# A fourth tile of score operands, the second half of a block loaded one patch sooner, and shared tiles that make room

## The chip, the cores and the metric

The kernel runs on one core of a Trainium2 chip. The metric is the device time of one execution in microseconds (us); for the kernel before it is the median of three executions.

A core has five engines that matter here: TensorE (PE, matrix products; PEld are its weight loads), VectorE (DVE), ScalarE (ACT), GpSimd (POOL) and SyncE (SP), which in this kernel only issues DMA transfers. Each engine takes its instructions strictly in order, and waits for other engines through semaphores. SyncE's queue issues nearly all transfers, so a transfer that has to wait there holds up all that stand behind it.

## The reference, cut to what matters

The input x has shape (8, 512, 2048), the context the same. A layer takes x through gated cross attention, then through a mixing of four streams:

```python
x = x + tanh(g_xattn) * xattn(layernorm(x), ctx, mask, ...)
x = x + tanh(g_ffn) * ffn(layernorm(x), ...)
```

The attention works on patches of 128 columns. Queries and keys both come from the normalized x, values from the context:

```python
q = einsum('ed,bdw->bew', Wq, qp) + bq      # per patch: 256 rows, 128 columns
k = einsum('ed,bdw->bew', Wk, qp) + bk
scores = einsum('bhdi,bhdj->bhij', qh, kh) / sqrt(32)   # 8 heads of 32 rows
attn = softmax(where(mask, scores, -1e9))
o = gelu(einsum('bhij,bhdj->bhdi', attn, vh))
out = (Wo @ o + bo) * mask
```

The mixing normalizes every row again, takes 24 logits per row from it, runs 50 Sinkhorn iterations on a 4 x 4 matrix per row, and combines the four 512-wide streams of the row with that matrix and with one 512 x 512 product.

## The kernel before, in words

**Tiling.** The 2048 columns of each of the 8 batches are cut into blocks of 512 columns (n = 0 to 31 over all batches), a block into 4 patches of 128 (p = 0 to 3, t = 4n + p), and, for the score operands, into two halves of 256 columns (m = 2n and 2n + 1). A half serves two patches.

**The score operands.** `proj(n)` (L261) normalizes a block, and computes queries and keys on TensorE in four groups of 128 rows (L288 to L290). ACT and DVE split each group into a high and a low half-precision part `ev` (L294, L295), and SyncE writes it to a scratch tensor `qd` in memory (L296). `stack(m)` (L301) loads one half back into a tile QK in the layout that the score products want: three transfers (L308 and twice L313, 768 KB together) and one row of the mask (L318). There are NS = 3 such tiles; half m goes to tile m mod 3, so its load waits until the scores of half m - 3 have been read. Three more rows of each tile are constants or row maxima: the constants are written once in the setup from `crow` (L401 to L404), the maxima by a small transfer per patch (L359, `mh`).

**The scores.** `smax(t)` (L339) multiplies queries and keys of patch t (L346, 8 matmuls), takes row maxima on DVE (L349 to L352), transposes them (L354), and writes them back into the QK tile (L356, L359). `expo(t)` (L626) makes the transposed scores with the maxima subtracted (L633, called sT) and ACT takes the exponential (L635). `attv(t)` (L638) multiplies with the values (L650, L654), which `vproj` (L328) makes from the context (`ct`, L326; L336). `outp(n)` (L660) takes a finished block through Gelu, the mask tile `mb` (L668, L669), a transposed copy `gT` (L672, L673, L679, L680) that is summed with weights into `g4` (L683) and `g4s` (L685), the output product (L705 to L708), the residual (L709) and the store to x1s (L712).

**The mixing.** `rawmap(b)` (L717) turns the sums of a finished batch into logits (among it `las`, L740, L741, and its transposes `lt`, L744), `ffn` runs the Sinkhorn iterations on DVE and POOL (L878 to L899), `mixv` combines the streams on ACT, POOL and DVE (L947 to L992; it passes products in the single buffer `pj`, L961, L984), and `mixp` does it on TensorE for fifteen of the 32 row groups (L995 to L1050), all after the main loop (the tail). Its four output tiles per group, `wp`, alternate between one buffer `eh` and two of `e32` (L1048), and are stored through ACT's queue (L1050).

**What sets the order.** The main loop runs over t, and for each t over the letters of ORDER. At each letter `act` (L1084) emits a piece of work. `smax` runs four patches ahead of `expo`. `stack(2(n+2))`, the first half of block n + 2, is emitted at p = 3 of block n just after the last group of its projection (L1138, L1139); `stack(2(n+1)+1)`, the second half of block n + 1, at p = 2 of block n (L1103, L1104). These calls give a priority; a scheduler with a model of the time line then fixes each engine's order of instructions when the kernel is built. It moves instructions past each other where tiles and semaphores allow. So a small edit can move instructions on all engines. Pools of tiles limit it: where a pool has one buffer for a tag, the next tile of that tag waits for the last reader of the one before.

The lines named are those of the kernel before.

Of the kernel before, what the change touches and what calls it, by code (L numbers as in the profile page):

```python
# [9 lines left out]
F32 = mybir.dt.float32  # L10
F32R = mybir.dt.float32r
F16 = mybir.dt.float16
# [7 lines left out]
P = 128  # L20
D = 512
S = 2048
DK = 256
NH = 8
DH = 32
BLK = 512
NBLK = S // BLK
NP = BLK // P
SB = 256
NSB = BLK // SB  # L30
PSB = SB // P
NS = 3
HI = 1000
XPRE_POOL = lambda b: b < 7
AHEAD = 3
# [26 lines left out]
BUF_W = 2  # L62
BUF_X1 = 2
BUF_PJ = 1
BUF_PH = 1
BUF_EP = 2
# [32 lines left out]
def gated_xattn_mhc_kernel(  # L99
# [21 lines left out]
    V, A, G, T, SY = nc.vector, nc.scalar, nc.gpsimd, nc.tensor, nc.sync  # L121
# [24 lines left out]
    WqkH = ctile([P, 4, 512], F16, "WqkH")  # L146
    WqkL = ctile([P, 4, 512], F16, "WqkL")
    Wv = ctile([P, 4, DK], F32, "Wv")
# [4 lines left out]
    Wm = ctile([P, 16, 32], F32, "Wm")  # L153
# [9 lines left out]
    maskT = ctile([P, B * 16], F32, "maskT")  # L163
# [27 lines left out]
    ep = ctx.enter_context(tc.tile_pool(name="ep", bufs=BUF_EP))  # L191
# [6 lines left out]
    VF = [ctile([P, 2, DK], F32, f"VF{i}") for i in range(NV)]  # L198
# [164 lines left out]
    with tc.tile_pool(name="set", bufs=1) as st:  # L363

        def stile(shape, dt, name, tag=None):
            return st.tile(shape, dt, tag=tag or name, name=name)
# [31 lines left out]
        ctload(0)  # L398
        SY.dma_start(bvc, bv.rearrange("(g p) -> p g", p=P))
        for val, rows in ((NEG, [t[96:97] for t in QS]), (-M_UNIT, [r for t in KS for r in (t[97:98], t[98:99])])):  # L400
            crow = stile([1, NH, SB], F16, f"crow{int(val)}")  # L401
            V.memset(crow, val)
            for r in rows:
                SY.dma_start(r, crow)  # L404
        tgx = stile([P, 1], F32, "tgx")
        A.activation(tgx, gx, AF.Tanh)
        A.activation(tgf, gf, AF.Tanh)
# [91 lines left out]
        pj = proj(1)  # L499
# [60 lines left out]
    lnp = ctx.enter_context(tc.tile_pool(name="lnp", bufs=3))  # L560
    op_ = ctx.enter_context(tc.tile_pool(name="op", bufs=BUF_OP))
    gp = ctx.enter_context(tc.tile_pool(name="gp", bufs=BUF_GP))
    fp = ctx.enter_context(tc.tile_pool(name="fp", bufs=2))
# [96 lines left out]
    def outp(n):  # L660

        b, k = divmod(n, NBLK)
        o = ob.pop(n)
        for g in range(2):
            gi = A.activation(o[:, g], o[:, g], AF.Gelu, bias=bvc[:, g : g + 1])
        with tc.issue_after(gi.ins), tc.high_priority():
            A.preload_act_table_set(EXP_SET)
        mb = gp.tile([P, BLK], F32, tag="mb", name="mb")  # L668
        SY.dma_start(mb, mask[b, k * BLK : (k + 1) * BLK].partition_broadcast(P))  # L669
        G.tensor_tensor(o, o, mb.unsqueeze(1).broadcast_to([P, 2, BLK]), ALU.mult)  # L670
        j0 = n * NP
        gt_ = op_.tile([P, NP, DK + 1], F32, tag="gT", name="gT")  # L672
        G.tensor_copy(gt_[:, :, DK], maskT[:, j0 : j0 + NP])  # L673
        yield
        for q in range(2):
            pt = ps_t.tile([P, 2, 2, P], F32, tag="t", name="gTp")
            for j in range(2):
                for e in range(2):
                    T.transpose(pt[:, j, e, :], o[:, e, (2 * q + j) * P : (2 * q + j + 1) * P], ident)  # L679
            V.tensor_copy(gt_[:, 2 * q : 2 * q + 2, 0:DK], pt.rearrange("p j e s -> p j (e s)"))  # L680
        g4 = ps_t.tile([P, DK + 1], F32, tag="t", name="g4")
        for p in range(NP):
            T.matmul(g4[32 * p : 32 * p + 32, :], Wm[:, k * NP + p, :], gt_[:, p, :], start=True, stop=True)  # L683
        if k == 0:
            g4s = lnp.tile([P, DK + 1], F32, tag="g4s", name="g4s", bufs=2)  # L685
            V.tensor_copy(g4s, g4)
            G4[b] = g4s
        else:
            V.tensor_tensor(G4[b], g4, G4[b], ALU.add)
        mr = MR[n % 2]  # L690
        SY.dma_start(mr[0:6, :], mrow_d[:, n * BLK : (n + 1) * BLK])
        gh = gp.tile([P, 2, BLK], F32R, tag="gh", name="gh")
        A.copy(gh, o)
        gl = gp.tile([P, 2, BLK], F32R, tag="gl", name="gl")
        G.tensor_tensor(gl, o, gh.bitcast(F32), ALU.subtract)  # L695
        if k == 0:
            sq2[b] = lnp.tile([P, 4, NBLK], F32, tag="sq2", name="sq2")
            x1s[b] = x1d.tile([D, S], F32, tag="x1s", name="x1s")
        xt = xtile.pop(n)
        yield  # L700
        for c in range(4):
            ps = ps_p.tile([P, BLK], F32, tag="p", name="op")
            cs = slice(c * P, (c + 1) * P)
            for e in range(2):
                T.matmul(ps, WoH[:, e, cs], gh[:, e], start=(e == 0), stop=False)  # L705
                T.matmul(ps, WoH[:, e, cs], gl[:, e], start=False, stop=False)  # L706
                T.matmul(ps, WoL[:, e, cs], gh[:, e], start=False, stop=False)
            T.matmul(ps, bo6[:, cs], mr, start=False, stop=True)  # L708
            V.tensor_tensor(xt[c], ps, xt[c], ALU.add)  # L709
            jk = fp.tile([P, BLK], BF16, tag="ph", name="junk2", bufs=BUF_PH)  # L710
            A.activation(jk, xt[c], AF.Square, bias=nmean[b][:, c : c + 1], accum_out=sq2[b][:, c, k : k + 1])  # L711
            defer(D_X1, "x1", lambda cs=cs, c=c: SY.dma_start(x1s[b][cs, k * BLK : (k + 1) * BLK], xt[c]))  # L712
            yield
# [3 lines left out]
    def rawmap(b):  # L717

        gtp = ps_t.tile([P, 3, 32], F32, tag="t", name="gtp")
        for e in range(2):  # L720
            T.matmul(gtp[:, e, :], G4[b][:, e * P : (e + 1) * P], sel, start=True, stop=True)
        T.matmul(gtp[0:3, 2, :], G4[b][:, DK : DK + 1].broadcast_to([P, 3]), sel, start=True, stop=True)
        gth = f1.tile([P, 2, 32], F32R, tag="gth", name="gth")
        V.tensor_copy(gth, gtp[:, 0:2, :])
        gtl = f1.tile([P, 2, 32], F32R, tag="gtl", name="gtl")
        V.tensor_tensor(gtl, gtp[:, 0:2, :], gth.bitcast(F32), ALU.subtract)
        ch3 = f1.tile([3, 32], F32R, tag="ch3", name="ch3")
        V.tensor_copy(ch3, gtp[0:3, 2, :])
        cl3 = f1.tile([3, 32], F32, tag="cl3", name="cl3")
        V.tensor_tensor(cl3, gtp[0:3, 2, :], ch3.bitcast(F32), ALU.subtract)  # L730
        V.tensor_scalar(cl3, cl3, cs3[:, 1:2], None, ALU.mult)
        c3 = f1.tile([3, 32], F32R, tag="c3", name="c3")
        V.scalar_tensor_tensor(c3, ch3.bitcast(F32), cs3[:, 0:1], cl3, ALU.mult, ALU.add)
        la = ps_t.tile([32, 512], F32, tag="t", name="la")
        for e in range(2):
            T.matmul(la, gth[:, e, :], WoH[:, e, :], start=(e == 0), stop=False)
            T.matmul(la, gth[:, e, :], WoL[:, e, :], start=False, stop=False)
            T.matmul(la, gtl[:, e, :], WoH[:, e, :], start=False, stop=False)
        T.matmul(la, c3, bor, start=False, stop=True)
        las = ep.tile([P, 512], F32, tag="eh", name="las", bufs=1)[0:32, :]  # L740
        A.copy(las, la)  # L741
        lt = ps_t.tile([P, 4, 32], F32, tag="t", name="lt")
        for c in range(4):
            T.transpose(lt[:, c, :], las[:, c * P : (c + 1) * P], ident[:32, :32])  # L744
        rw = lnp.tile([P, 4, 34], F32, tag="raw", name="raw")
        V.tensor_tensor(rw[:, :, 0:32], lt, rawx[b], ALU.add)
        V.tensor_reduce(rw[:, :, 32], sq2[b], AX.X, ALU.add)
        V.tensor_copy(rw[:, :, 33], nmean[b])
        raws[b] = rw
# [245 lines left out]
    def mixp(b, n, maps, inp=False):  # L995
# [9 lines left out]
        for g in range(4):  # L1005
            q = 4 * n + g
# [10 lines left out]
        pt = (ps_t if inp else ps_p).tile([P, 4, P], F32, tag="t" if inp else "p", name="xpT")  # L1017
# [25 lines left out]
        for g in range(4):  # L1043
            q = 4 * n + g
            ps = ps_t.tile([P, 512], F32, tag="t", name="mx1") if inp else pw[g // 2][:, g % 2]
            T.matmul(ps, QD[:, 32 * g : 32 * g + 32].rearrange("p t i -> p (t i)"), ys, start=True, stop=False)  # L1046
            T.matmul(ps, HD[:, g].rearrange("p t i -> p (t i)"), xc[g], start=False, stop=True)  # L1047
            w = fp.tile([P, 512], F32, tag="w", name="w", bufs=BUF_W) if inp else ep.tile([P, 512], F32, tag="eh" if g % 2 else "e32", name="wp", bufs=1 if g % 2 else BUF_EP)  # L1048
            A.activation(w, ps, AF.Identity, bias=rec[:, q, 2:3])
            A.dma_start(orow[q * P : (q + 1) * P, :], w)  # L1050
            yield 1

    NT_ = NTOT * NP
    mixq, tailq = [], []
# [29 lines left out]
    def act(c, t):  # L1084
        n, p = divmod(t, NP)
# [12 lines left out]
        elif c == "P" and live_ and n + 1 < NTOT:  # L1098
            if p == 0:
                at("proj", run, pj_[0])  # L1100
            if (SP0 == 0 or n == 0) and p == 0:
                at("stack", stack, NSB * (n + 1))
            if p == 2:  # L1103
                at("stack", stack, NSB * (n + 1) + 1)  # L1104
        elif c == "l" and live_:
            if p == LXP and n > 1 and n + 3 < NTOT:
# [127 lines left out]
```

## Time and profile before

| what | value |
|---|---|
| median of three executions | 1650.96 us (1650.79 to 1660.62) |
| the profiled execution | 1660.9 us |
| its span, first to last instruction | 1659.1 us |
| granted clock of TensorE, mean | 0.966 |
| busy: TensorE, DVE, ACT, POOL | 1481.3, 1160.3, 1061.5, 798.7 us |
| bytes moved by DMA | 330.55 MB, mean 199 GB/s |

The profile comes from one further execution. Busy time of an engine is the time in which it carried out an instruction; the rest it waited. A line such as `PE smax L346 <- DMA QK<-qd: 21.5, 12, 5.8` says that TensorE's instruction of line 346, which writes the tile smax, had to wait for the transfer that fills QK from qd: 21.5 us in all, 12 times, 5.8 us at the longest. In a time line the columns are start (us from the span's start), duration, engine, line, operation, tiles and shapes, count, and in square brackets the engine's idle time before it and what ended it. Lines of SPq are issues: their duration is that of the issue, not of the transfer.

### The profile page before, as it was taken

How to read it: one execution, taken by the hardware profiler on the slowest of the kernel's cores; microseconds unless marked ns; L12 is line 12 of the kernel's file. 1: busy time of each engine (PE TensorE's matmuls, PEld its weight loads, DVE VectorE, ACT ScalarE, POOL GpSimd, SP SyncE). 2: the span in 40 equal slices, each digit the busy share in tenths (PEclk: the TensorE clock that was granted, in tenths of full speed). 3: DMA queues.
4: the chain of work that ended last, by engine and by line, in shares of the span. 5: the costliest groups of instructions: out<-in, count | busy, mean ns of one | idle time of the engine just before them, and what ended most of it. 6: DMA issues, size and time to landing. Idle time of an engine off the chain costs nothing.

```text
span 1659.1 us, 31662 instructions
## 1 busy us (share of the span) xinstructions
PE 1481.3 (89%) x10524; PEld 887.6 (53%) x10589; DVE 1160.3 (70%) x3513; ACT 1061.5 (64%) x1924; POOL 798.7 (48%) x1149
## 2 busy tenths in 40 slices
PE   4798999999999988989897998888899999699998
PEld 2455556665656655555554565555565656433333
DVE  7454434665677578867886788876898878678772
ACT  3357466767667666777677766686677665655564
POOL 1321423444554454646675664667567744433221
PEclk8999999999999999999998998999999999899999
DMA  5688886687568755986678756896566565154653
GB/s 192 154 248 247 251 280 186 179 255 231 169 204 233 241 178 167 257 266 198 176 225 241 226 177 182 240 280 191 160 178 200 165 190 141 53 169 153 184 167 134
DMA packets 258179, 330.55 MB, mean 199 GB/s; under 512 B 43543, under 2 KB 143191, under 8 KB 258014
## 3 DMA queue, kind: packets, MB, share of 16 engines
q1 hardware_dynamic: 248078, 312.44, 63.7%
q10 hardware_dynamic: 9936, 16.06, 2.6%
q8 instruction: 84, 1.38, 0.4%
q14 instruction: 81, 0.66, 0.1%
HBM read 226.71 MB, written 101.16 MB: 198 GB/s over the span
## 4 chain that ended last, share of the span: by engine, by line
PE 36%; DMA 20%; DVE 18%; ACT 11%; issue 8%; POOL 6%; SPq 2%; POOLq 0%; ACTq 0%; another core or an unknown queue 0%; DVEq 0%
DMA xs<-in_x_dram 4%; DMA QK<-qd 4%; DMA xTt<-in_xT_dram 3%; PE vp L336 3%; DVE w L988 3%; PE mx L1046 3%; DMA qd<-ev 3%; PE mx L1047 3%; DVE smax L349 2%; PE op L705 2%; PE qk L288 2%; PE xpp L1012 2%; PE qk L289 2%; PE qk L290 2%; DMA out_dram<-w 2%
## 5 line engine op out<-in xcount | busy, mean ns | idle before, releaser
L336 PE MATMUL vp<-Wv,ct 128*128 128x256 f32 x1024 | 249.0, 398 | 15.2 <-DMA ct<-in_cx_dram 7.8
L336 PEld LDWEIGHTS vp<-Wv,ct 128*128 128x128 f32 x1024 | 202.3, 201 | 49.8 <-issue 9.9
L888 POOL TENSOR_TENSOR W<-E,uv 128x64 f32<-128x64 f32 x343 | 117.4, 346 | 203.3 <-DVE uv L886 100.4
L288 PE MATMUL qk<-xh,WqkH 128*128 128x512 f16 x512 | 196.1, 384 | 13.2 <-DVE ev L295 8.3
L349 DVE TENSOR_REDUCE smax<-smax 128x8 f32<-128x1024 f32 x128 | 155.8, 1217 | 65.0 <-PE smax L346 63.6
L276 POOL TENSOR_TENSOR xl<-xn,xh 128x512 f16<-128x512 f32 x126 | 153.9, 1221 | 97.3 <-ACT xh L274 92.3
L289 PE MATMUL qk<-xl,WqkH 128*128 128x512 f16 x512 | 196.3, 383 | 3.9 <-POOL xl L276 3.9
L290 PE MATMUL qk<-xh,WqkL 128*128 128x512 f16 x512 | 196.2, 383 | 0.0
L882 POOL TENSOR_TENSOR W<-E,uv 128x64 f32<-128x64 f32 x308 | 106.7, 350 | 175.0 <-DVE uv L892 76.0
L635 ACT ACTIVATE e<-sT,ebi,esc 128x1024 f32<-128x1024 f32 x128 | 153.2, 1197 | 40.4 <-PE sT L633 40.1
L988 DVE SCALAR_TENSOR_TENSOR w<-x,Et,w 128x512 f32<-128x512 f32 x153 | 151.1, 989 | 22.6 <-POOL w L986 11.9
L271 POOL TENSOR_SCALAR xn<-xt,ln_r,nb 128x512 f32<-128x512 f32 x126 | 107.9, 856 | 117.5 <-DVE nb L255 53.1
L890 DVE TENSOR_REDUCE sm<-W 128x16 f32<-128x64 f32 x392 | 99.7, 257 | 83.5 <-POOL W L888 79.5
L711 ACT ACTIVATE junk<-xt,nmean 128x512 bf16<-128x512 f32 x128 | 91.6, 716 | 76.1 <-DVE xt L709 41.6
L705 PE MATMUL op<-gh,WoH 128*128 128x512 f32 x256 | 117.3, 460 | 24.9 <-DVE ev L295 12.4
L294 ACT ACTIVATE ev<-qk,bqs 128x512 f16<-128x512 f32 x128 | 86.4, 676 | 75.8 <-PE qk L290 75.4
L346 PE MATMUL smax<-QK 97*128 97x128 f16 x1024 | 84.4, 225 | 45.9 <-DMA QK<-qd 26.2
L295 DVE SCALAR_TENSOR_TENSOR ev<-qk,bqs,ev 128x512 f16<-128x512 f32 x128 | 93.2, 729 | 42.9 <-ACT ev L294 34.4
L709 DVE TENSOR_TENSOR xt<-op,xt 128x512 f32<-128x512 f32 x128 | 86.5, 676 | 37.0 <-remote 20.6
L884 DVE TENSOR_REDUCE sm<-W 128x16 f32<-128x64 f32 x352 | 73.1, 211 | 56.0 <-POOL W L882 52.5
L346 PEld LDWEIGHTS <-QK 97*128 97x128 f16 x1024 | 67.2, 100 | 76.2 <-DMA QK<-qd 33.4
L706 PE MATMUL op<-gl,WoH 128*128 128x512 f32 x256 | 103.7, 405 | 0.2 <-POOL gl L695 0.2
(288 smaller groups left out, 3451.6 us busy)
## 6 DMA issues: line engine op xcount, KB each, us to landing
xt<-in_x_dram SPq DMA_DIRECT2D x64, 512.0 KB
ct<-in_cx_dram SPq DMA_DIRECT2D x64, 512.0 KB
qd<-ev SPq DMA_DIRECT2D x128, 256.0 KB
QK<-qd SPq DMA_DIRECT2D x64, 512.0 KB
xTt<-in_xT_dram SPq DMA_DIRECT2D x64, 512.0 KB
x1s<-xt SPq DMA_DIRECT2D x128, 256.0 KB
xs<-in_x_dram SPq DMA_DIRECT2D x56, 512.0 KB
x<-x1s SPq DMA_DIRECT2D x34, 512.0 KB
```

Of the source, the lines that this page charges most:

```text
L271: G.tensor_scalar(xn, xt[c], rstd1[b][:, c : c + 1], nb1[b][:, c : c + 1], ALU.mult, ALU.add)
L276: (V if n == 0 and c > 1 else G).tensor_tensor(l, xn, h, ALU.subtract)
L288: T.matmul(ps, WqkH[:, c, ms], hs[c], start=(c == 0), stop=False)
L289: T.matmul(ps, WqkH[:, c, ms], ls[c], start=False, stop=False)
L290: mm = T.matmul(ps, WqkL[:, c, ms], hs[c], start=False, stop=(c == 3))
L336: T.matmul(ps[:, h, :], ct[:, c, h * P : (h + 1) * P], Wv[:, c, :], start=(c == 0), stop=(c == 3))
L346: T.matmul(sc[:, h, :], q[0:97, h, sl], kk[0:97, h, sl], start=True, stop=True)
L349: V.tensor_reduce(mx, sc, AX.X, ALU.max)
L635: A.activation(e32, sc, AF.Exp, bias=ebi[:, t : t + 1], scale=esc[:, t : t + 1])
L705: T.matmul(ps, WoH[:, e, cs], gh[:, e], start=(e == 0), stop=False)
L888: (G if SK_POOL(b - B + 8) else V).tensor_tensor(W4[:, h], E4[:, h], ub[:, h], ALU.mult)
L988: V.scalar_tensor_tensor(w, x1[j], E[:, n, 4 * j + i : 4 * j + i + 1], w, ALU.mult, ALU.add)
```

## The change

The kernel after has four QK tiles instead of three, so half m goes to tile m mod 4 and waits for half m - 4. The second half of a block is emitted at p = 1 instead of p = 2. A QK tile takes 8 KB of every partition, and the room for the fourth is made in these places:

- `crow` is one row of 256 columns, and the transfer repeats it for the 8 heads;
- `gT` is cut in two tiles of two patches each; the second shares the buffer of `mb`, which grows by 8 bytes a partition;
- `g4s` has one buffer instead of two;
- `las` uses the buffer of `pj`;
- the tag `eh` is gone: `mixp` writes its outputs in turn to five tiles that the main loop no longer needs (parts of the weights WqkH, WqkL and Wv, and both value tiles VF) and to two buffers of `e32`.

```diff
-NS = 3
+NS = 4
...
-            crow = stile([1, NH, SB], F16, f"crow{int(val)}")
+            crow = stile([1, SB], F16, f"crow{int(val)}")
             V.memset(crow, val)
             for r in rows:
-                SY.dma_start(r, crow)
+                SY.dma_start(r, crow.unsqueeze(1).broadcast_to([1, NH, SB]))
...
-        mb = gp.tile([P, BLK], F32, tag="mb", name="mb")
+        mb = gp.tile([P, 2 * (DK + 1)], F32, tag="mb", name="mb")[:, :BLK]
         SY.dma_start(mb, mask[b, k * BLK : (k + 1) * BLK].partition_broadcast(P))
         G.tensor_tensor(o, o, mb.unsqueeze(1).broadcast_to([P, 2, BLK]), ALU.mult)
         j0 = n * NP
-        gt_ = op_.tile([P, NP, DK + 1], F32, tag="gT", name="gT")
-        G.tensor_copy(gt_[:, :, DK], maskT[:, j0 : j0 + NP])
+        gt_ = [op_.tile([P, 2, DK + 1], F32, tag="gT", name="gT"), gp.tile([P, 2, DK + 1], F32, tag="mb", name="gT1")]
+        for q in range(2):
+            G.tensor_copy(gt_[q][:, :, DK], maskT[:, j0 + 2 * q : j0 + 2 * q + 2])
...
-            V.tensor_copy(gt_[:, 2 * q : 2 * q + 2, 0:DK], pt.rearrange("p j e s -> p j (e s)"))
+            V.tensor_copy(gt_[q][:, :, 0:DK], pt.rearrange("p j e s -> p j (e s)"))
...
-            T.matmul(g4[32 * p : 32 * p + 32, :], Wm[:, k * NP + p, :], gt_[:, p, :], start=True, stop=True)
+            T.matmul(g4[32 * p : 32 * p + 32, :], Wm[:, k * NP + p, :], gt_[p // 2][:, p % 2, :], start=True, stop=True)
         if k == 0:
-            g4s = lnp.tile([P, DK + 1], F32, tag="g4s", name="g4s", bufs=2)
+            g4s = lnp.tile([P, DK + 1], F32, tag="g4s", name="g4s", bufs=1)
...
-        las = ep.tile([P, 512], F32, tag="eh", name="las", bufs=1)[0:32, :]
+        las = fp.tile([P, 512], F32, tag="pj", name="las", bufs=BUF_PJ)[0:32, :]
...
-            w = fp.tile([P, 512], F32, tag="w", name="w", bufs=BUF_W) if inp else ep.tile([P, 512], F32, tag="eh" if g % 2 else "e32", name="wp", bufs=1 if g % 2 else BUF_EP)
+            w = fp.tile([P, 512], F32, tag="w", name="w", bufs=BUF_W) if inp else tailw(g)
...
+    spare = [WqkH.bitcast(F32)[:, 0:2, :], WqkL.bitcast(F32)[:, 0:2, :], Wv[:, 0:2, :], VF[0], VF[1]]
+    turn = [0]
+
+    def tailw(g):
+        k = turn[0] % (len(spare) + 2)
+        turn[0] += 1
+        if k < len(spare):
+            return spare[k].rearrange("p c e -> p (c e)")
+        return ep.tile([P, 512], F32, tag="e32", name="wp")
...
-            if p == 2:
+            if p == 1:
                 at("stack", stack, NSB * (n + 1) + 1)
```

## The prediction, made before the changed kernel had run

> **What bounds the kernel now.** I read the page first, then the waits of TensorE and of SyncE's queue, then the time line of single blocks on both.
>
> ```profile
> span 1659.1 us, 31662 instructions
> PE 1481.3 (89%) x10524; PEld 887.6 (53%) x10589; DVE 1160.3 (70%) x3513; ACT 1061.5 (64%) x1924; POOL 798.7 (48%) x1149
> ...
> PEclk8999999999999999999998998999999999899999
> ```
>
> TensorE is busy for 89% of the span, so the change can only win what lies in its 178 us of idle time, and lose what it adds there. The windows by 100 us put 35 us of that idle time into the first 100 us, about 123 us into 100 to 1400, 14 us around 1400 to 1500 and nearly none into the tail. In 100 to 1400 the waits of TensorE are these (us, times, longest):
>
> ```profile
> PE smax L346 <- DMA QK<-qd: 21.5, 12, 5.8
> PE op L705 <- DVE ev L295: 12.4, 10, 2.5
> PE g L683 <- DVE gT L680: 9.1, 6, 3.3
> PE lgx L577 <- DMA xTt<-in_xT_dram: 8.8, 6, 4.5
> ```
>
> The largest is the wait for the score operands, which the change is about. SyncE's queue waits for the same tiles, because a tile must be free before it is loaded (over the whole span):
>
> ```profile
> SPq L308 <- DMA qd<-ev: 32.1, 24, 3.8
> SPq L308 <- PE sT L633: 26.2, 12, 5.4
> SPq L313 <- PE sT L633: 16.1, 11, 3.5
> ```
>
> Which half of a block is waited for? The time line of SyncE, then of TensorE, around the longest such wait:
>
> ```profile
> 902.70 0.64 SPq L308 DMA_DIRECT2D QK<-qd  x1
> 903.38 0.59 SPq L313 DMA_DIRECT2D QK<-qd  x1
> 904.07 0.39 SPq L326 DMA_DIRECT2D ct<-in_cx_dram  x1
> 904.55 0.93 SPq L612 DMA_DIRECT2D xs<-in_x_dram  x2
> 910.42 0.62 SPq L308 DMA_DIRECT2D QK<-qd  x1
> 911.09 1.07 SPq L313 DMA_DIRECT2D QK<-qd  x2
> ```
> ```profile
> 908.52 1.01 PE L346 MATMUL smax<-QK 97*128 97x128 f16 x8 [5.76 <-DMA QK<-qd]
> 909.33 1.06 PE L633 MATMUL sT<-QK 99*128 99x128 f16 x8
> ...
> 926.07 0.61 PE L346 MATMUL smax<-QK 97*128 97x128 f16 x8 [0.68 <-ACT e L635]
> ```
>
> The first half (issue at 902.70) stops TensorE for 5.76 us. The second half is issued at 910.42, just after the sT group at 909.33 has freed its tile, and its first smax starts at 926.07, 15.6 us later and not held by that load. I paired every L308 issue with the first smax group of its tile in this way. All waits of smax for QK<-qd lie at first halves. From block 4 on, first halves start 5.5 to 10.5 us after the issue (13 of 28 under 6.6), second halves 7.8 to 19.9 us (mean 13.1). A load alone lands in 5.5 to 6 us, so every second half already has at least 2 us to spare.
>
> **The change part by part.** The profiled execution took 1660.9 us (span 1659.1 and 1.8 around it), 0.6% over the median of 1650.96; the terms below are a few us, so I take them off the median unscaled.
>
> *Second half a patch sooner, fourth tile.* TensorE's waits at second halves come to 0.3 us (one, for the mneg row at 681.7). Gain: 0 to 0.3, taken as 0. The freed queue time (26.2 + 16.1 + 6.8 for L318, 49 us of SyncE standing at a load until sT frees a tile) is SyncE's: what stood behind it has slack (mh rows below). Zero.
>
> What the loads move past: in the built programs I counted what stands on SyncE between the first and the second half's L308. Before: 34 ct, 29 x1s, 14 xs, 14 MR, 14 out, 11 xTt, 11 mb, 10 x1, 6 qd, 4 mh. After: 15 x1s, 8 xTt, 6 out, 6 x1, 3 mh. So some 110 transfers now come behind three more issues (0.63 + 2 x 0.50 = 1.6 us) and 768 KB (3.8 us at the page's 199 GB/s). ct is waited for once only, in the setup; xs costs ACT 33.0 us in 19 waits, and 14 x 3.8 = 53 us more at the very most, on an engine that is 64% busy; TensorE's waits for ACT's e after it are 4.9 us. I take 0, bound +5.
>
> What stands ahead of the first half: those waits depend on it. With 260 to 522 KB issued in the 6 us ahead, first halves landed after 5.8 us (t=80, 32, 112, 120); with 1542 KB after 8.95 (t=64): 3.1 us per 1000 KB. With 1664 KB issued in the 3 us *behind* it (t=80) it still took 5.83, so the second half behind the first doesn't slow it. Between the last qd write and the first half's L308 stand 504 KB on average before and 414 after; in the four issues ahead of that write 1053 and 989. That is 90 to 150 KB less, 0.3 to 0.5 us on each of the 16 blocks in which TensorE waits there: 4.5 to 7.5 us. Only part reaches the end, since DVE's waits follow: -3, bounds -8 to +8 (the order may as well put more in front; other waits are re-dealt too).
>
> On this point the Trainium skill ("DMA: Bandwidth & Descriptors", section "Queues, rings and completion order") says that on each DMA engine a queue's descriptors are consumed in ring order. It speaks against the change: the 768 KB moved up don't go any faster and everything behind has to let them by. By the rule alone the first half gains nothing from a sooner second half and the sum would have 0 for -3; t=80 agrees that what is behind doesn't matter.
>
> TensorE's own order hardly moves: priced by the mean time of each line, the work between a block's last projection matmul and the first smax at p=0 is 15.1 us before and 14.9 after. So the cover of the first half is as thin as it was.
>
> *Setup.* Two memsets of 2048 columns (1.765 us each) become 256 (0.22 by ratio): 3.1 us less on DVE before 5.3 us; but the last x tile is waited for until 18.4. DVE's order also changes: wq is scaled before the last statistics, and WqkL (4.73) stands ahead of the chain to nb (0.9). ACT's WqkH (4.76) starts at 22.0 to 23.6 instead of 25.24; WqkL ends 31.5 to 33.1 instead of 34.76; then nb, xn 0.77, xl 1.15: first L289 at 34.3 to 35.9 instead of 35.63, since POOL's xl no longer runs beside WqkL (4.31 then, 1.15 elsewhere). Taken -0.5; bounds -2 and +2 (WqkH no sooner: the chain waits for WqkL). Three more constant rows: 3 x 0.55 us on SyncE, which is idle from 33 to 43.9. Zero.
>
> *Two gT tiles, one in mb's buffer.* 32 more copies on POOL at 0.19: 6 us on an engine 48% busy, covered by it; bound +6. The next mask load now waits for the g matmuls instead of o's multiply, which end 8.4 us later on average (3.9 to 14.2). It stands a little later on SyncE; behind it is mostly mh (20 of the next two rows in the loop). From block 4 to the last but one, mh is issued 13 to 47 us ahead of its sT; that covers 8.4. Zero; without that cover it is the time of the rival below.
>
> *g4s with one buffer:* rawmap has read it a block earlier. Zero, at worst 8 copies of 0.42. *las in pj's buffer:* of the 8 copies three would find pj in use (616.04 until 617.47, 800.18 until 803.47, 991.22 until 991.79); with las 0.57 long, the transposes at 802.36 would start 1.7 us later and the others about in time. Taken +1, bounds 0 and +5.
>
> *Tail output in seven buffers instead of three:* ACT waits 9.4 us for its own output transfers, TensorE 3.5 (weight loads) for ACT; but the windows 1500 to 1600 show TensorE busy for 100 of 100. Only the last 10 us can win: -1, bounds 0 and -3.5.
>
> Sum: 0 - 3 - 0.5 + 1 - 1 = -3.5, so 1650.96 - 3.5 = 1647.5 us. Within 1% is about what a measurement can't tell from no change: 1634.5 to 1667.5.
>
> **The rivals.**
> *Faster:* the waits at first halves go as well, because the scheduler uses the fourth tile to have first halves loaded ahead. For: they are TensorE's largest wait (21.5 in the loop, 4.6 in the setup). Against: they end with the qd write (SPq L308 <- DMA qd, 24 times), which the change leaves where it is. 1650.96 - 26.1 = 1625 us.
> *Slower:* the first half lands later. The re-dealt queue puts more transfers ahead of the L308 of first halves, or keeps the mask load waiting at the head of SyncE in front of it. Against: 414 KB for 504. For: every queue's order is new, and 1000 KB cost 3.1 us in each of 31 blocks, with no cover. It decides from +170 KB, 0.53 us a block, 16.5 us; with +250 KB 24 us: 1675 us.
> *It does nothing* is nearly my forecast: 1651.
>
> **How the numbers follow.** Forecast case (with "nothing") 0.68, own range 1639 to 1656 from the bounds; faster rival 0.15; slower rival 0.17. Of each rival 0.03 stays within 1%. So faster 0.12, same 0.74, slower 0.14. For 8 in 10 the range goes into both rivals: 1632 to 1665.
>
> **What would show it.** Right: smax at p=2 as free of QK waits as before; waits at p=0 still 15 to 25 us; SPq L308 <- PE sT gone; the tail unchanged at about 186 us of TensorE from the first xpp; first L289 near 35. Wrong: QK waits of TensorE under 8 us (faster) or over 40, or a new wait at smax, sT or vp for mh, ct or ACT's e of over 10 us in all (slower).

## The result and the profile after

The kernel after takes 1715.31 us (median, 1706.27 to 1718.11) where the kernel before took 1655.79 us in the same session: ratio 1.035, 95% interval 1.028 to 1.041. It is slower, outside the predicted range (1632 to 1665) and beyond the slower rival (1675). The two profiled executions lie 45.3 us apart (1704.4 for 1659.1), less than the medians: that of after was the fastest of its four.

The first lines of the page of after, and then TensorE's and SyncE's waits in the same stretches as shown of before (what waited, for what: us in all, times, longest):

```profile
span 1704.4 us, 31858 instructions
PE 1519.9 (89%) x10589; PEld 893.0 (52%) x10589; DVE 1162.4 (68%) x3513; ACT 1063.0 (62%) x1924; POOL 793.7 (47%) x1181
...
PEclk7989999999999999999999998999999999799999
```
```profile
PE smax L346 <- DMA QK<-qd: 23.2, 11, 4.0
PE op L706 <- DVE ev L295: 20.0, 14, 3.5
PE smax L354 <- DVE mq L352: 9.2, 6, 3.5
PE lgx L577 <- DMA xTt<-in_xT_dram: 9.0, 6, 3.4
PE g L684 <- DVE gT L681: 7.5, 4, 3.5
```
```profile
SPq L313 <- DMA qd<-ev: 59.5, 29, 5.6
SPq L308 <- DMA qd<-ev: 36.9, 24, 3.1
SPq L318 <- PE sT L633: 30.2, 15, 5.4
SPq L313 <- PE sT L633: 9.6, 6, 2.8
```

The line `SPq L308 <- PE sT L633` (26.2 us before) is gone, but SyncE's queue is not freed. The row of the mask that belongs to each half (L318) now waits there for sT instead, 30.2 us for 6.8, and L313 waits longer for the qd writes (before):

```profile
SPq L313 <- DMA qd<-ev: 30.9, 17, 3.8
SPq L318 <- PE sT L633: 6.8, 6, 1.6
```

All waits at the three lines of a load (L308, L313, L318) sum to 166 us after and 140 us before. TensorE's wait for QK is about what it was (23.2 us for 21.5). SyncE's and TensorE's time line at t = 32, after:

```profile
381.40 0.65 SPq L308 DMA_DIRECT2D QK<-qd  x1
382.10 0.59 SPq L313 DMA_DIRECT2D QK<-qd  x1
382.74 0.61 SPq L308 DMA_DIRECT2D QK<-qd  x1
383.39 0.60 SPq L313 DMA_DIRECT2D QK<-qd  x1
```
```profile
387.17 0.61 PE L346 MATMUL smax<-QK 97*128 97x128 f16 x8 [3.97 <-DMA QK<-qd]
...
395.28 0.61 PE L346 MATMUL smax<-QK 97*128 97x128 f16 x8
...
401.21 0.62 PE L346 MATMUL smax<-QK 97*128 97x128 f16 x8
```

Both halves are now issued 1.3 us apart (7.0 us before, at the same block). The second half has 18.5 us until its first smax at 401.21, but the first half, issued no sooner after its qd write, still stops TensorE for 4.0 us. So the large transfers of the second half come sooner, as the change says, and that was worth nothing, as forecast. The time was lost elsewhere. I split each run at its first smax and its first xpp group:

| us | before | after | difference |
|---|---|---|---|
| start to first smax | 62.4 | 61.8 | -0.6 |
| loop (first smax to first xpp) | 1399.2 | 1433.8 | +34.6 |
| tail (first xpp to TensorE's last) | 191.8 | 203.3 | +11.5 |

No single wait accounts for the loop's 34.6 us. The windows of before and of after over the loop (length; busy time and count of PE, PEld, DVE, ACT, POOL; granted clock; DMA share; GB/s):

```profile
62.40:1461.60 1399.20, 1260.95 (x9808) 800.07 (x9875) 994.60 (x2920) 929.41 (x1702) 729.63 (x1033) 0.97 0.70 206
```
```profile
61.80:1495.60 1433.80, 1289.53 (x9873) 804.01 (x9873) 1004.03 (x2922) 931.66 (x1702) 727.88 (x1067) 0.96 0.68 200
```

TensorE idles 144 us for 138 (length less busy; 65 records are missing before, see the counts, so its true idle time is rather less), and is itself busy up to 29 us longer for the same work. Two things show in that. Summed over the records of the granted clock, half speed costs 59.7 us for 46.1 (25 stretches for 17; 24 of the 25 have a TensorE wait of 1.5 us or more close by, from 7 us ahead of their start to 3.5 behind it; of moments picked at random in the loop, three in ten do). And matmuls of 32 output rows, which run side by side on separate columns only while they are neighbours in TensorE's order (the tail below shows it), are split into more runs: u from VF 187 runs and 88.8 us for 171 and 82.7 (each run from its first matmul to the next other instruction); u from onesb, lgx and g 4.8 us more together. That is 6 + 13.6 + 10.9 = 30.5 of the 34.6 us, but it is a tally and not a proof. Half speed partly falls into idle time and is counted again where it lengthens the split matmuls. Among the six profiles below that keep the loop's order, its cost is 43 to 56 us, the 56 in one whose loop is no longer than before; and the room alone, below, has as many runs of u from VF as after (189, 87.3 us) and loses 10 us. The terms are sums over the whole loop: many small waits that lie elsewhere than before. The waits that grew most did so by 8 us (op for ev, 20.0 for 12.4) and 6 us (the transposed maxima for mq, 9.2 for 3.6).

### The profile page after: what moved, and what is told of

It reads as the page before. It is cut to its first block, busy times and chain, and to the rows that moved or that the text cites. A ratio compares the mean times of both kernels' runs of the same rounds, so it can differ in the third digit from the quotient of the medians.

```text
span 1704.4 us, 31858 instructions
## 1 busy us (share of the span) xinstructions
PE 1519.9 (89%) x10589; PEld 893.0 (52%) x10589; DVE 1162.4 (68%) x3513; ACT 1063.0 (62%) x1924; POOL 793.7 (47%) x1181
## 4 chain that ended last, share of the span: by engine, by line
PE 37%; DVE 19%; DMA 17%; issue 9%; POOL 7%; ACT 7%; SPq 1%; POOLq 0%; ACTq 0%; DVEq 0%
PE vp L336 4%; DMA xs<-in_x_dram 3%; DMA x<-x1s 3%; PE mx L1047 3%; PE mx L1048 3%; DVE w L989 3%; DVE smax L349 2%; DMA qd<-ev 2%; PE qk L288 2%; PE op L706 2%; PE xpp L1013 2%; DMA QK<-qd 2%; PE qk L289 2%; PE qk L290 2%; DMA xTt<-in_xT_dram 2%
## 5 line engine op out<-in xcount | busy, mean ns | idle before, releaser
L336 PE MATMUL vp<-Wv,ct 128*128 128x256 f32 x1024 | 249.2, 397 | 13.6 <-DMA ct<-in_cx_dram 6.8
L889 POOL TENSOR_TENSOR W<-E,uv 128x64 f32<-128x64 f32 x343 | 114.7, 338 | 221.7 <-DVE uv L887 128.3
L289 PE MATMUL qk<-xl,WqkH 128*128 128x512 f16 x512 | 198.1, 387 | 0.8 <-POOL xl L276 0.7
L883 POOL TENSOR_TENSOR W<-E,uv 128x64 f32<-128x64 f32 x308 | 103.0, 339 | 174.8 <-DVE uv L893 98.1
L635 ACT ACTIVATE e<-sT,ebi,esc 128x1024 f32<-128x1024 f32 x128 | 153.4, 1199 | 41.6 <-PE sT L633 41.5
L989 DVE SCALAR_TENSOR_TENSOR w<-x,Et,w 128x512 f32<-128x512 f32 x153 | 141.2, 923 | 40.7 <-POOL w L987 18.7
L346 PE MATMUL smax<-QK 97*128 97x128 f16 x1024 | 81.6, 219 | 30.3 <-DMA QK<-qd 24.7
L670 POOL TENSOR_TENSOR o<-o,mb 128x1024 f32<-128x1024 f32 x32 | 77.2, 2413 | 62.3 <-ACT o L665 62.0
```

The lines of the kernel that those rows point to most:

```text
L289: T.matmul(ps, WqkH[:, c, ms], ls[c], start=False, stop=False)
L336: T.matmul(ps[:, h, :], ct[:, c, h * P : (h + 1) * P], Wv[:, c, :], start=(c == 0), stop=(c == 3))
L635: A.activation(e32, sc, AF.Exp, bias=ebi[:, t : t + 1], scale=esc[:, t : t + 1])
L889: (G if SK_POOL(b - B + 8) else V).tensor_tensor(W4[:, h], E4[:, h], ub[:, h], ALU.mult)
L989: V.scalar_tensor_tensor(w, x1[j], E[:, n, 4 * j + i : 4 * j + i + 1], w, ALU.mult, ALU.add)
```

## The experiments

**Theory 1**: parts of the change that do no work in the loop make the scheduler deal out another order of all engines' instructions, and that order is slower; the tail is slower because of its new output buffers. **Rivals**: the fourth tile, the sooner load or the mask load behind the g matmuls cost by themselves. The order can be read from the built program, so most runs come with a count of the differences from the kernel compared. TensorE has 12253 instructions, but a count can exceed that (12353 below): read it as a measure of likeness, not as the number of instructions that moved. "Shift" is the first xpp of the one profiled execution against the 1461.6 us of before. Six profiles whose loops have the order of before, or nearly, lie between 1453.3 and 1465.2, so a shift is good to some 6 us.

**The order in the loop: the constant row**

```diff
-            crow = stile([1, NH, SB], F16, f"crow{int(val)}")
+            crow = stile([1, SB], F16, f"crow{int(val)}")
...
-                SY.dma_start(r, crow)
+                SY.dma_start(r, crow.unsqueeze(1).broadcast_to([1, NH, SB]))
```

> The kernel before, with the constant row alone made short (one row of 256 columns, repeated by the transfer). Three QK tiles, the second half at p = 2, all other tiles as before. The loop does the same work on the same buffers, but the scheduler deals out another order: the listing of TensorE's order differs in thousands of rows. Theory 1 (most of the loss is the order that the scheduler happens to deal when anything ahead of the loop changes): the first xpp 10 to 25 us later than 1461.6, the time 1661 to 1676, ratio 1.006 to 1.015. Rival (the loss comes from what the change does in the loop: sooner loads, the fourth tile, the mask load behind the g matmuls): nothing of that is here, so within 5 us of before, ratio 0.997 to 1.003, although the order is new.

Measured: ratio 1.022 (1.017 to 1.026), shift +35.5, tail 192.7. This one edit, in the setup, costs as much in the loop as the whole change, and more than I expected. TensorE's order is another one, in well over half of its places. To part the edit from the order, a padding of the setup's memsets:

```diff
+            pad = stile([1, 7 * SB], F16, f"pad{int(val)}")
             V.memset(crow, val)
+            V.memset(pad, val)
```

> As the run with the short constant row alone, but each short memset is followed by a second one of the other 1792 columns, into a tile that nobody reads, so that the setup on DVE is about as long as before. With that the built order of TensorE, ACT and POOL is the same as before, instruction for instruction; DVE has two more memsets, SyncE nine places of difference, all in the setup. Theory 1 (the 35 us of the short row come from the order of the loop that the scheduler deals out after a shorter memset): back to before, first xpp within 5 us of 1461.6, ratio 0.997 to 1.003. Rival (the short row itself costs on the chip: one row repeated by the transfer, another layout of the setup's tiles): 1690 to 1700 again, ratio 1.018 to 1.026.

Measured: ratio 1.000 (0.997 to 1.002), shift -6.7. The rival falls: the short row itself is free. Then the other way round, `12 * SB` for `7 * SB`:

> As the padded constant row, with a second memset of 3072 columns instead of 1792, so that the setup's memsets are longer than before, not shorter. The order that is built is nearly that of the run with the short row alone (of TensorE's 12253 instructions 101 stand otherwise, of SyncE's 1136 22), and not that of before. Theory 1 (the order sets the time): as the short row alone, first xpp 25 to 40 us later than 1461.6, ratio 1.016 to 1.025. Rival (what sets it is something that the short memset does at run time): back to before or a few us more, ratio 0.998 to 1.005.

Measured: ratio 1.025 (1.019 to 1.031), shift +42.2. With a longer memset, but nearly the order of the short one, the loss is there; it also comes at the same patches (at t = 16, 48, 80 and 96 the two runs are 16, 35, 20, 36 and 16, 44, 31, 45 us behind before). The windows of the padded row, the short row and the long memset over the loop:

```profile
61.60:1454.80 1393.20, 1261.90 (x9804) 798.53 (x9868) 994.33 (x2920) 930.07 (x1702) 732.31 (x1033) 0.97 0.70 207
```
```profile
62.50:1497.10 1434.60, 1287.57 (x9874) 804.99 (x9874) 1009.25 (x2934) 933.46 (x1703) 733.73 (x1040) 0.95 0.68 201
```
```profile
66.50:1503.80 1437.30, 1281.29 (x9808) 804.20 (x9873) 1015.86 (x2934) 933.64 (x1702) 735.30 (x1041) 0.95 0.68 200
```

Idle 131, 147 and 156 us (the first and the last lack 65 to 70 of TensorE's records, so theirs is rather less); clock 0.97, 0.95, 0.95. The loop's instructions are the same in all three, its tiles lie at the same addresses, and the setup differs by a memset: the order alone moves the loop by some 40 us. By the records of the clock, half speed costs 43, 65 and 68 us (part of which falls into idle time).

**Other parts alone**

```diff
-            if p == 2:
+            if p == 1:
```

> The kernel before with the second half of a block called at p = 1 instead of p = 2, three QK tiles and every other tile as before. The listing of TensorE's order differs from that of before in a few hundred rows only. Theory 1 (order, not loads): within 4 us of before. Rival (the sooner load itself costs, since it stands at the head of SyncE's queue): the second half waits there for the tile, SPq L308 <- PE sT grows from 26 to 40 us or more, what stands behind it comes later, and the time is 10 to 20 us longer.

Measured: ratio 0.999 (0.996 to 1.003), shift +3.6, `SPq L308 <- PE sT L633` 27.8 us. TensorE's order is that of before: the tile is not free sooner, so the scheduler leaves the load about where it was. With three tiles the sooner call is next to nothing.

```diff
-        las = ep.tile([P, 512], F32, tag="eh", name="las", bufs=1)[0:32, :]
+        las = fp.tile([P, 512], F32, tag="pj", name="las", bufs=BUF_PJ)[0:32, :]
```

> The kernel before with las in the buffer of pj alone. TensorE's order is that of before for 2270 of 12253 instructions; behind, 8374 stand otherwise. Theory 1 (another order dealt out at random against one that was good): nothing in the first 15% of the loop, then a loss of 5 to 40 us, ratio 1.003 to 1.024. Rival 1 (las waits for pj, or pj for las, as the prediction had it): 0 to 5 us, at the eight places of las only. Rival 2 (new orders are as often better as worse): a gain is as likely as a loss.

Measured: ratio 1.014 (1.011 to 1.018), shift +22.4. Until t = 64 the run is within 5 us of before; then it falls behind in steps. ACT does wait for lt to give pj free (8.7 us in 5 waits), and once 4.7 us for POOL ahead of las; how much of the 22 us is that and how much the order, this run does not show.

The cut gT (two tiles of `[P, 2, DK + 1]`, the second with the tag of mb, as in the diff of the change):

> The kernel before with gT cut in two tiles, the second in the buffer of mb; nothing else. Theory 1 (new order): first xpp 5 to 40 us later, ratio 1.003 to 1.024, and SyncE's wait at the mask load is longer but nobody waits for what stands behind it. Rival (the mask load that waits for the g matmuls holds up mh and the other loads): TensorE's waits for mh (sT), ct, xTt and QK together grow by 15 us or more against 38 us before, ratio 1.01 to 1.02.

Measured: ratio 1.021 (1.017 to 1.025), shift +23.3. TensorE's waits for QK, xTt and mh, and SyncE's at the mask load:

```profile
PE smax L346 <- DMA QK<-qd: 27.9, 12, 5.9
PE lgx L577 <- DMA xTt<-in_xT_dram: 12.7, 11, 4.3
PE smax L346 <- DMA QK<-mneg_d: 6.1, 1, 6.1
PE sT L633 <- ACT mh L356: 5.2, 3, 3.5
```
```profile
SPq L669 <- PE g L684: 22.1, 15, 2.8
SPq L669 <- DVE gT L681: 21.8, 10, 9.6
```

These TensorE waits sum to 51.9 us; the same sum before is 41.5 (26.2, 9.3, 0.3, 5.7; my "38" was too low). SyncE stands at the mask load for 44 us in these lines, but it stood there for 36 us before too (16.1, 15.0 and 5.0, for POOL), and TensorE's wait for mh did not grow (5.2 us for 5.7). Loads grew by 10.4 us as TensorE's waits, 6.1 of them at a single patch; a cost of the shared buffer of up to 10 of the 23 us is not excluded.

```diff
-NS = 3
+NS = 4
...
-    WbL = ctile([P, 4, 512], F16, "WbL")
+    WbL = WbH
...
-            g4s = lnp.tile([P, DK + 1], F32, tag="g4s", name="g4s", bufs=2)
+            g4s = lnp.tile([P, DK + 1], F32, tag="g4s", name="g4s", bufs=1)
...
-            if p == 2:
+            if p == 1:
```

> The kernel before with the fourth QK tile and the second half at p = 1, and none of the change's room edits but g4s. The room is made by letting WbL share the tile of WbH, so that the mixing's product is computed with other weights (same instructions, sizes and, but for 128 of TensorE's places, the same order). Built with p = 2 instead, TensorE's order differs in 4 of 12253 places, so the sooner call is all but without effect. Theory 1 (another order is what counts): first xpp 5 to 45 us later than before, tail 190 to 194 us, ratio 1.003 to 1.027. Rival 1 (the fourth tile costs by itself, as all orders with four tiles so far lost 34 us or more in the loop): 34 to 52 us later, ratio 1.02 to 1.032. Rival 2 (the fourth tile helps and the room edits lose it): 0 to 20 us sooner, ratio 0.988 to 1.

Measured: ratio 1.037 (1.033 to 1.040), shift +47.3, tail 193.6; wait of smax for QK 28.3 us over the whole span (26.2 before). This kernel leaves the low half of one set of weights out of the mixing; its instructions and their sizes are those of the full work. The order is new over most of the loop. The fourth tile does not help the wait that it is about; rival 2 falls. Between the order and a cost of the tile itself this run cannot tell.

The kernel after with `p == 2`, and with `NS = 3` as well:

> The kernel after with the second half at p = 2 again: fourth tile and all of the room, without the sooner load. TensorE's order is that of the changed kernel for the first 7226 of 12253 instructions and another one behind. Theory 1 (order and tail): first xpp 20 to 45 us later than before, tail 200 to 204 us, the time 1690 to 1720, ratio 1.019 to 1.037. Rival (the sooner load is what costs): the loop back near before, first xpp 1458 to 1470, and with the longer tail 1655 to 1675, ratio 0.998 to 1.01.

> The kernel after with three tiles and the second half at p = 2: only the room is made, the score operands are as before. TensorE's order is new from instruction 159 on. Theory 1: one more new order; first xpp 10 to 45 us later than before, tail 200 to 204 us, the time 1680 to 1720, ratio 1.013 to 1.037. Rival (the fourth tile and the sooner load cost by what they put on SyncE's queue): only the tail is left, first xpp 1458 to 1468, the time 1655 to 1672, ratio 0.998 to 1.009.

Measured: four tiles with p = 2, ratio 1.027 (1.023 to 1.031), shift +38.8, tail 200.7. Room alone, ratio 1.016 (1.012 to 1.019), shift +10.1, tail 201.4. The sooner load is not the main cause: without it the loss stays, though this call, too, changes the order (from TensorE's instruction 7226 on). The room alone loses in the loop too, but less than any other new order so far.

**Does the fourth tile cost beside its order?** More orders of the same kernels, made by a second memset behind the constant row as above (`7 * SB` or `1 * SB` in after, then `1 * SB` and `7 * SB` in the room alone):

> The kernel after with the padded constant row: all of the change is there, and the setup is as long as before. TensorE's order is another one than that of the kernel after from instruction 359 on (8401 of 12253 stand otherwise). Theory 1 (the loss is that of the order, not of the four tiles and the sooner load): the time moves by 5 to 30 us against the kernel after, either way; tail 200 to 205 us; ratio to before 1.005 to 1.04. Rival (four tiles and the sooner load cost the 34 us of the loop): within 5 us of the kernel after, first xpp 1491 to 1501, ratio 1.03 to 1.04.

> The kernel after with a second memset of 256 columns behind each constant row (into a tile that nobody reads): the whole change in a third order (8601 of TensorE's 12253 places differ from the kernel after; 1115 from the padded one, so it should be near that). Theory 1: near the padded one, first xpp 40 to 60 us later than before, ratio 1.027 to 1.04. Rival (orders scatter widely even where they are alike): anything between 1.0 and 1.04.

> Room alone (three tiles, p = 2), with a second memset of 256 columns behind each constant row: 9933 of TensorE's 12253 places differ from the first run of the room alone. If the fourth tile costs beside the order: first xpp 5 to 25 us later than before, under all four-tile orders so far (29 to 52). If it is the order alone: 25 to 45 us later is as likely.

> Room alone (three tiles, p = 2), with a second memset of 1792 columns: 2080 of TensorE's 12253 places differ from the first run of the room alone, 12353 lines from the second order. If the fourth tile costs beside the order: first xpp 5 to 25 us later than before. If it is the order alone: near the first run of the room alone (10 us) by its likeness, but 25 to 45 us is possible.

| loop order | ratio (95%) | shift |
|---|---|---|
| after | 1.035 (1.028 to 1.041) | +34.0 |
| after, second order (7) | 1.034 (1.030 to 1.037) | +51.8 |
| after, third order (1) | 1.029 (1.025 to 1.033) | +29.2 |
| room alone, three tiles | 1.016 (1.012 to 1.019) | +10.1 |
| room alone, second order (1) | 1.024 (1.020 to 1.028) | +32.1 |
| room alone, third order (7) | 1.018 (1.015 to 1.022) | +23.5 |

The second order of after moved by 18 us and the third lies 23 us under the second, though their orders are alike (1115 places): orders scatter. Over the new orders so far, three tiles lose 10 to 42 us in the loop, four tiles 29 to 52. The shifts overlap, but the averages (room alone 22, after 38) leave room for some 16 us that the fourth tile itself may cost. The ratios say it more clearly: among the kernels that make the room and keep after's tail they are 1.016 to 1.024 with three tiles and 1.027 to 1.035 with four. So the order alone is probably not the whole loss. One thing that sets the two apart is SyncE's queue: its waits at the three lines of a load sum to 124 to 151 us under the new orders with three tiles and to 154 to 166 us under those with four. What TensorE loses by that is not shown; it stays open.

**The tail**

```diff
-            w = fp.tile([P, 512], F32, tag="w", name="w", bufs=BUF_W) if inp else ep.tile([P, 512], F32, tag="eh" if g % 2 else "e32", name="wp", bufs=1 if g % 2 else BUF_EP)
+            w = fp.tile([P, 512], F32, tag="w", name="w", bufs=BUF_W) if inp else tailw(g)
```

> The kernel before with the seven output buffers of the tail alone. The main loop's order is nearly that of before. Theory 1 (the freer buffers change ACT's order in the tail, xc comes one at a time, and so the xpp matmuls come in 37 runs for 31, each run 0.98 us whatever its length): TensorE from the first xpp to its end 200 to 204 us for 191.8, the first xpp within 3 us of 1461.6, the time 8 to 12 us longer, ratio 1.005 to 1.007. Rival (the tail of the changed kernel is longer because of what the main loop hands it, and more buffers do no harm): 190 to 193 us, the time 0 to 3 us shorter.

Measured: tail 200.1 us, first xpp 1459.4, ratio 1.003 (1.000 to 1.007). With the loop's order kept, the seven buffers alone lengthen the tail by 8.3 us. ACT waits no more for its output transfers (7.3 us in the tail before), and the scheduler deals out the tail in another order, in which the matmuls of xpp come in 37 runs for 31 (20 singles for 6). A pair, from the time line of before, and a single matmul, from that of this run (a matmul is two records):

```profile
1565.46 1.05 PE L1012 MATMUL xpp<-xc,PD 128*32 128x512 f32 x4
1566.44 1.13 PE L1046 MATMUL mx<-xo,QD 128*128 128x512 f32 x2
```
```profile
1565.42 1.05 PE L1012 MATMUL xpp<-xc,PD 128*32 128x512 f32 x2
1566.40 0.39 PE L945 MATMUL yp<-WbH,plb 128*128 128x512 f16 x1
```

Both hold TensorE for 0.98 us: a matmul alone costs what two cost side by side, so six runs more are 6 x 0.98 = 5.9 us (the busy time of xpp is 40.8 us for 34.2). The Trainium skill ("TensorE: Matmul & The Clock Gate", section "Part 3: Packing small matmuls — row/col tiling") says that matmuls on different column groups run at the same time, and that a pack takes one matmul's time plus about 4 ns for each further tile. The traces agree for neighbours: from the start of a group to the next instruction it takes 0.98 us for one or two, 0.99 for three and 1.00 for four together. Here an instruction in between ends the group. So the cure is to issue the four together:

```diff
-            T.matmul(xps[32 * g : 32 * g + 32, :], PD[:, g, :], t, start=True, stop=True)
             xc.append(t)
+        m3 = T.matmul(xps[96:128, :], PD[:, 3, :], xc[3], start=True, stop=True)
+        with tc.issue_after(m3.ins), tc.high_priority():
+            for g in range(3):
+                T.matmul(xps[32 * g : 32 * g + 32, :], PD[:, g, :], xc[g], start=True, stop=True)
```

> The kernel before with the four xpp matmuls of a group issued one after another, once the last xc is ready (15 runs of four for 31 runs of one, two and four); nothing else. Theory (a run of these matmuls costs 0.98 us on TensorE whatever its length, as they run side by side on separate columns only while they are neighbours in the order): 16 runs less, 16 x 0.98 = 15.7 us of TensorE in the tail; from the first xpp to the end about 176 to 182 us for 191.8, the time 10 to 16 us shorter, ratio 0.990 to 0.994. Rival (the 0.98 us is only how the ends are modelled, or ACT sets the pace of the tail): the tail within 2 us of 191.8, or longer, since the first three matmuls now wait for the fourth xc.

Measured: ratio 0.999 (0.996 to 1.002), tail 189.2 us. xpp falls to some 17 us as expected, but the time does not: with three output buffers, ACT now waits for them. A wait of ACT from 1490 us on, and TensorE's waits in the tail:

```profile
ACT wp L1052 <- DMA out_dram<-wp: 32.4, 12, 4.2
```
```profile
PE mx L1049 <- ACT xo L1033: 7.3, 8, 1.8
PE xpp L1013 <- ACT xc L1011: 2.8, 1, 2.8
PE mx L1049 <- ACT wp L1052: 1.6, 2, 1.5
```

So the two tail edits should need each other:

> The kernel before with both tail edits: seven output buffers, and the four xpp matmuls of a group one after another. With three output buffers the grouping saved 15.5 us of TensorE's time in the tail, but ACT then waited 32 us for output transfers to free a buffer, and TensorE's mx for ACT. Theory (the two edits need each other): xpp again near 16.6 us in 15 runs, ACT's wait for its own output transfers under 3 us, TensorE from the first xpp to its end 174 to 181 us for 191.8, the time 11 to 18 us shorter than before, ratio 0.989 to 0.994. Rival (another limit stands right behind, such as the xc loads or ACT's copies of xo): 186 to 192 us, ratio 0.996 to 1.001.

Measured: ratio 0.991 (0.988 to 0.994), tail 181.7 us; ACT's wait for output transfers is gone, and one group of four stands in the time line as

```profile
1566.16 0.62 PE L1013 MATMUL xpp<-xc,PD 128*32 128x512 f32 x1
1566.17 0.63 PE L1016 MATMUL xpp<-xc,PD 128*32 128x512 f32 x3
...
1567.16 1.13 PE L1049 MATMUL mx<-xo,QD 128*128 128x512 f32 x2
```

The tail is just above what was expected (174 to 181); the time is the lowest of the study, and lower than both kernels. In the kernel after the same edit:

> The kernel after with the four xpp matmuls of a group one after another. The order of the loop is that of the kernel after, the tail has seven output buffers and 15 runs of xpp instead of 37. Theory: the tail goes from 203.3 to 176 to 184 us, as with both tail edits on the kernel before (181.8); the loop stays at 1495 +- 5; so 20 to 26 us less than the kernel after, ratio to before 1.018 to 1.024. Rival (the tail of the changed kernel is long because of what the loop leaves over for it): 190 us or more.

Measured: ratio 1.018 (1.012 to 1.025), tail 179.1 us for 203.3, first xpp 1497.8. The tail's loss was the split, not what the loop left over. Last, the u matmuls together too (the eight with VF under a high priority, on top of the fastest kernel):

> The fastest kernel so far (seven output buffers, xpp together) with the eight u matmuls of a patch put one after another as well (128 runs of them in the order instead of 143); 5461 of TensorE's 12253 places differ. Theory 1 (a new order costs more than the grouping wins): u<-e,VF 75 to 80 us instead of 83, but first xpp 5 to 30 us later than in that kernel, ratio to before 0.994 to 1.01. Rival (the split groups are the main part of what new orders cost): first xpp 5 to 8 us sooner, ratio 0.984 to 0.989.

Measured: ratio 0.994 (0.992 to 0.997); u with VF 77.6 us for 83.2, but the first xpp is at 1464.1 for 1453.3. The grouping won 5.6 us of TensorE's time, and the loop seems to have given it back and more; but 10.8 us is within the spread of 12 us, and the intervals of the two ratios overlap. Against the kernel before, this loop is within the spread too, the only widely different order that is. So the split of u may have a part in what new orders cost, though in the others it is 0 to 6 us.

## Why the prediction was wrong, point by point

- **"TensorE's own order hardly moves: priced by the mean time of each line"**: this step failed. It priced one stretch by line means, in which an order cannot show: neither which matmuls are neighbours, nor which wait falls where, nor the half-speed stretches that stand beside waits. The order was new over most of the kernel. A new order by itself cost some 40 us where nothing else differed (the constant row), and the three-tile kernels with new orders, but for the last run's, lost 10 to 42 us. That is enough to cover the loop's +34.6 us; how much of it is the order's and how much the fourth tile's (some 16 us by the averages) no run parts.
- **"-1, bounds 0 and -3.5" for the tail**, and "tail unchanged": failed, with the sign. It gave +11.5 in the changed kernel, +8.3 alone. The forecast said what a wait removed would win and never asked what ACT does with its freedom; "below nothing" was excluded without a reason.
- **Setup, -0.5**: right in size (first smax -0.6) by luck. The working did not come true: ACT's WqkH started at 24.73 us where 22.0 to 23.6 was forecast, and the first L289 at 37.30 where 34.3 to 35.9 was (35.63 before), since the chain to nb waited for WqkL, as only the bound of +2 allowed. The time came back later, where the first smax waited 1.6 us for QK instead of 4.6. And it left out the main thing: the 3.1 us less of memset reorder the loop.
- **Second half sooner, 0; freed queue time, 0**: the zero for the sooner half held as far as the runs show (alone 0.999). The queue time, though, was not freed: of the 49.1 us at a load until sT is done 39.8 are left, most of them now at L318, and the waits for qd grew.
- **First half, -3**: in 100 to 1400, where its 16 blocks lie, the wait went from 21.5 to 23.2 us. The gain did not come; +1.7 is inside the bounds. (Over the whole span it is 24.7 for 26.2, because of the one wait in the setup.)
- **110 transfers behind the load, 0**: TensorE's wait for ct went from 7.8 to 6.8 us and ACT's for xs from 33.0 to 28.9; only xTt grew, from 9.3 to 13.1, inside the bound of 5.
- **gT and the mask load, 0 with a price as in the rival**: alone +23.3 us of shift, up to 10 of it by later loads; the rest I put down to the order, which this run does not show apart.
- **las, +1, bounds 0 and 5**: alone +22.4, outside the bounds; the waits of ACT that belong to it are 8.7 + 4.7 us, already more than the +1 taken; how much of them reached the end, and how much is the new order, is open.
- **g4s, 0**: no run shows it alone.
- **The rivals**: the faster one (first-half waits vanish) did not happen in any run. The slower one had the wrong mechanism: QK's wait did not grow.
- **The chances**: 0.74 for "same" came from summing small terms with the order taken as neutral. Of twelve loop orders that differ widely from before, the changed kernel's among them, eleven lost 10 us or more and none won. (Some are alike, and some carry edits that may cost by themselves.)

## What to carry to other kernels

When a scheduler with a model of time fixes the order, first compare the built orders: an edit that leaves them alone can be priced by its parts, one that re-deals them must be priced as a new draw, and a kernel whose order has proved good seems to stand to lose (here 10 to 52 us of 1660 in eleven of twelve orders). Pad what an edit shortens in the setup, and see whether the order comes back, before giving the edit itself a price. Matmuls that share the array by columns should be issued as one group, and a wait that is taken away should be followed to what its engine does next.

## What the runs showed of the hardware that was not expected

- An f32 matmul of 32 output rows and 512 columns holds TensorE for 0.98 us alone, and two or three neighbours together for 0.98 to 0.99 us (the xpp of the tail). Another instruction in between ends the group, and the next matmul costs 0.98 us again: 31 runs have 34.2 us of busy time, 37 runs 40.8.
- Half-speed stretches stand beside short waits of TensorE: 17 stretches (92 us long) in the loop of before, 25 (120 us) in after, 29 (143 us) in its padded order. They vary without a new order too: 85 to 113 us in the six profiles with the order of before. The Trainium skill ("TensorE: Matmul & The Clock Gate", section "Why this matters for your kernels") advises no idle gaps over about 3 us. Here waits of 1.5 to 2.5 us, single or close together, stand beside half-speed stretches too (in after, only 14 of the 25 have a wait of 2.5 us or more close by).
